# Gelus behind their additions, three products for the last batch's first pair, and a new order ahead of the branch and at the end

## The chip, the core and the metric

The kernel runs on one core of a Trainium2 chip. The time is the device time of one execution in microseconds (us). Before the change it is 1835.79 us, the median of three runs (1835.6 to 1835.98). One execution was also taken with the hardware profiler; that one took 1836.18 us, and its span, from the first to the last instruction, is 1834.4 us, so 1.8 us lie around the span. Five engines work side by side, each through its own instructions in order: PE (matrix products; PEld is its weight loading), DVE (vector work), ACT (activation functions), POOL (a second, slower vector engine), SP (which here only starts DMA transfers).

## The reference

The layer takes `x` of 4 batches, 2048 tokens and 256 features. What is computed:

```python
def step(h, qkv):                       # a linear recurrence over the tokens, per head (16 heads of 64)
    q, k, v = qkv
    h = alpha[None, :, :, None] * h + k[:, :, :, None] * v[:, :, None, :]
    return (h, jnp.einsum('bhi,bhij->bhj', q, h))
...
o = o * gate                            # gate = silu(xn @ Wg.T + bg)
y = o.reshape(batch, seq_len, D_INNER) @ WO.T + bO
...
x = _layernorm(x + attention(x))        # attention adds x once more
gf = _global_net(x.mean(axis=1))        # one number for each batch
out = x
for _ in range(3):                      # cycles
    tf = sigmoid(gelu(gelu(gelu(out @ w1 + b1) @ w2 + b2) @ w3 + b3) @ w4 + b4)     # one number a token
    coupling = 0.1 + adaptive_range * (0.7 * gf + 0.3 * tf - 0.5) * 2.0
    out = out + coupling * twist(out)   # twist: the four quarters of the features changed about, two with a minus
x = _layernorm(x + out)
```

Since the first product of the net is linear and the coupling is one number for each token, the kernel keeps u = out @ w1 and v = twist(out) @ w1, and a cycle becomes u + c v and v - c u, without a new product with w1.

## The kernel before, in words

**Ahead of the branch** (lines 230 to 329). Inputs are loaded; the bias of V is spread over all partitions by a product (line 248) that ACT copies out (line 249); a Sigmoid on ACT gives the decay factors (`powers[0]`, line 257), which DVE doubles up to 64 powers (`double`, lines 259 to 266); the first 512 tokens are normalised (`norm_steps`: `rs` on POOL, `xh` on DVE, transposes on PE line 182, ACT line 184); four products make V (`values_of`, line 199, added up on DVE line 203); the decay table `dtok` is transposed on PE (line 320) and copied on ACT (line 324); a one-element product (line 308) gives a flag that says whether a fast form of the recurrence is safe. Every engine reads the flag and branches. With these inputs the fast program runs.

**The fast program's loop** (`fast_program`). Batches of 2048 tokens are cut into 4 groups of 512 tokens, groups into 8 pairs of heads: 128 iterations, each in the same order on PE: 16 products for the outputs (`products`, line 1161), 16 for the state (`updates`, 646), three projections K, Q, g of the iteration after next (480), then a slot, then `inter` (1144), `all_scores` (573), `keys` (630), mostly one product for V (199), then a second slot. ACT copies the scores out (`copy_first`, line 589, "the A copies"), DVE copies a masked part (`copy_own`, line 594) and then `products` can start. On POOL each iteration has three multiplications (526, 536, 540) behind the Q projection.

**The slots** (`between`). Everything behind the recurrence is cut into steps and put into these slots by a planner when the program is built, from three clocks of its own (`clock`, `takes`) and the times written at each `step`: output projection and layer norm (`post`, queue `posts`), the global net (`nets`), and the coupling net (`feed_forward`, queue `couples`), which treats two groups at a time, s = 0 and 1. Small pieces of DVE work that belong to a product are put on the list `late` and issued at the end of a slot (`late_work`).

**The coupling net.** For all batches but the last, `both(s)` makes u and v with three products a half o instead of four (line 847): with J the twist, w1m = w1[0] + w1j[0], and the two differences of the halves of x1T formed on DVE (lines 841, 842), u and v are the first product (copied by ACT, line 848) plus the second and plus the third (DVE, lines 851, 852, in `adds`, on the list `late`). A step of its own, `gelu` (line 899), then issues two Gelus for both halves. In the last batch both pairs of groups take `first` (line 823): four products for u and four for v. `layer2` (line 905), w3 (940), w4 with a tanh (949, 952) follow; the result `cs` holds the coupling of each token on all partitions, and `turn` starts with c = cs ar3 + shift (868) and updates u and v. In the last batch's turn of cycle 1, DVE updates u (875, 878) while POOL updates v (876, 880). In cycle 2 only u is updated (886, 891).

**The end** (`the_end`). What is left of the queues after the loop is issued in the order of the string `AT_THE_END`: o is `post`, n the global net, p and q the last batch's first and second pair of groups, v the second pair's `first_twisted`. The last step of a pair mixes the token-wise couplings into coefficients (lines 970 to 993, a power on POOL line 987) and forms the output from them (ACT 1002, DVE 1016) for the DMA.

ACT's function tables are switched by an ACT_TABLE_LOAD, put in by the compiler where the next function is in another set: Gelu and Silu are, here; copies, Identity and Tanh need no switch of their own.

Of the kernel before, what the change touches and what calls it, by code (L numbers as in the profile page):

```python
# [49 lines left out]
P = 128  # L50
# [6 lines left out]
C = 64  # L57
# [10 lines left out]
ORDERED = {mybir.EngineType.PE, mybir.EngineType.DVE, mybir.EngineType.Activation, mybir.EngineType.Pool}  # L68


AT_THE_END = "qoopooqnnqnpqppvppqvqqqpqppqqpqqpqppqpppppqqqpqpqqqqpqpqpppqqpqpppqpppqqqpqqqqqq"
STAGES = ((2, 4), (8, 4), (32, 2))
EPS = 1e-5
LOW_ALPHA = 2.0**-5
# [4 lines left out]
def post_norm_layer(ctx: ExitStack, tc: tile.TileContext, a: dict, out: bass.AP):  # L79
# [152 lines left out]
    with ExitStack() as first:  # L232
        first.enter_context(tc.manual_schedule(engines=ORDERED))
        work = first.enter_context(tc.tile_pool(name="first", bufs=1))
        psum = first.enter_context(tc.tile_pool(name="firstp", bufs=4, space=bass.MemoryType.PSUM))

        def bank():
            return psum.tile([P, 512], F32, tag="pf", name="pf")


        diag = work.tile([P, HP, P], F32, tag="diag", name="diag")
        nc.vector.tensor_mul(
            diag, ident.unsqueeze(1).to_broadcast([P, HP, P]), b_in["V"].unsqueeze(2).to_broadcast([P, HP, P])
        )
        for half in range(2):
            hps = slice(half * (HP // 2), (half + 1) * (HP // 2))
            pt = bank()
            nc.tensor.matmul(pt, ones, diag[:, hps, :].rearrange("p j i -> p (j i)"), start=True, stop=True)
            nc.scalar.copy(bVt[:, half * 512 : (half + 1) * 512], pt)


        nc.vector.memset(up[:, :, 0:1], 1.0)
        nc.vector.memset(down[:, :, C : C + 1], 1.0)
        high = work.tile([P, 6], F32, tag="high", name="high")
        nc.vector.memset(high, 0.0)
        powers = [work.tile([P, HP, 1], F32, tag=f"apow{i}", name="apow") for i in range(C.bit_length())]
        nc.scalar.activation(powers[0], logit.unsqueeze(2), AF.Sigmoid)
# [26 lines left out]
        for i in range(3, C.bit_length() - 1):  # L284
            double(i)
        nc.vector.tensor_copy(up[:, :, C : C + 1], powers[-1])
        nc.vector.tensor_copy(down[:, :, 0:1], powers[-1])

        two = work.tile([P, HP, 2, C], F32, tag="two", name="two")
        nc.vector.tensor_copy(two, down[:, :, 1 : C + 1].unsqueeze(2).to_broadcast([P, HP, 2, C]))  # L290
        square(4, w_in["K"].rearrange("p k o -> p (k o)"))
        values_of(bank(), xn0, V0, 0, 0)

        peak = work.tile([P, 1], F32, tag="peak", name="peak")
        nc.vector.tensor_reduce(
            peak, w_in["Q"].rearrange("p k o -> p (k o)"), AX.X, ALU.max, apply_absolute_value=True
        )
# [12 lines left out]

        nc.vector.tensor_copy(kf[:, :, 0 : M + 1], down[:, :, C - M : C + 1])
        nc.vector.tensor_copy(qf[:, :, M:H], up[:, :, 0:M])
        nc.vector.reciprocal(kf[:, :, M + 1 : H], up[:, :, 1:M])
        nc.vector.reciprocal(qf[:, :, 0:M], down[:, :, C - M : C])
        values_of(bank(), xn0, V0, 0, 3)
        for half in range(2):
            hps = slice(half * (HP // 2), (half + 1) * (HP // 2))
            pt = bank()
            for j in range(HP // 2):
                nc.tensor.transpose(  # L320
                    pt[:, j * P : (j + 1) * P],
                    two[:, half * (HP // 2) + j].rearrange("p c s -> p (c s)"), ident,
                )
            nc.scalar.copy(dtok[:, hps, :].rearrange("p j i -> p (j i)"), pt)  # L324


        nc.gpsimd.iota(trow, pattern=[[1, C]], base=0, channel_multiplier=0)
        nc.gpsimd.iota(scol, pattern=[[0, 1]], base=0, channel_multiplier=1)
        nc.vector.tensor_scalar(scol, scol, C - 1, None, ALU.bitwise_and)
# [5 lines left out]
    def layer(fast, inside):  # L335
# [448 lines left out]
        def feed_forward(b, g0):  # L784
# [19 lines left out]
            gs = (g0, g0 + 1)  # L804
            u, v = [], []
            h1, h2 = {}, {}
            done = {}

            ctok = []
# [21 lines left out]
            def both(s):  # L831
# [11 lines left out]
                for o in range(2):  # L843
                    at = yield step("pe", 2.58, act=0.6)
                    ps = [pj() for _ in range(3)]
                    for w, r, q in ((w1m, o_, ps[0]), (w1[:, 0, :], diff, ps[1]), (w1j[:, 0, :], p_, ps[2])):
                        nc.tensor.matmul(q, w[:, o * P : (o + 1) * P], r, start=True, stop=True)  # L847
                    nc.scalar.copy(us[:, o, :], ps[0])

                    def adds(o=o, ps=ps):  # L850
                        nc.vector.tensor_add(vs[:, o, :], ps[1], us[:, o, :])
                        nc.vector.tensor_add(us[:, o, :], ps[2], us[:, o, :])

                    late.append(adds)
                    late.append(lambda: None)

                done["u", s] = at + 1.6
                done["v", s] = done["u", s]
                yield from gelu(s)

            def first_twisted():
                for s in range(2):
                    yield from first(s, w1j, v, "v")

            def turn(s, cycle):

# [2 lines left out]
                by_token(s, cycle - 1)  # L869
                if cycle == 1 and end:  # L870

                    done["u", s] = yield step("dve", 2.6)
                    ts = [(new("t"), SPARE[g0].pop(0)) for o in range(2)]
                    for o, (t0, t1) in enumerate(ts):
                        nc.vector.tensor_mul(t0, cs[s], v[s][:, o, :])
                        nc.gpsimd.tensor_mul(t1, cs[s], u[s][:, o, :])
                    for o, (t0, t1) in enumerate(ts):
                        nc.vector.tensor_add(u[s][:, o, :], u[s][:, o, :], t0)
                    for o, (t0, t1) in enumerate(ts):
                        nc.gpsimd.tensor_sub(v[s][:, o, :], v[s][:, o, :], t1)  # L880
                    return
                for o in range(2):
                    done["u", s] = yield step("dve", 1.3)
                    uo, vo = u[s][:, o, :], v[s][:, o, :]
# [10 lines left out]
            def gelu(s):  # L895
                done["h1", s] = yield step("act", 1.4, delay=0.2, at=lambda: done["u", s])
                for o in range(2):
                    h1[s, o] = new("h1")
                    nc.scalar.activation(h1[s, o], u[s][:, o, :], AF.Gelu, bias=b1[:, o : o + 1])

            def layer2(s):
                done["h2", s] = yield step("pe", 1.75, act=0.7, at=lambda: done.get(("h1", s), 0.0))
# [464 lines left out]
```

## Time and profile before

| what | value |
|---|---|
| time, median of 3 | 1835.79 us |
| the profiled execution's own time | 1836.18 us |
| its span | 1834.4 us |
| PE busy | 1781.6 us, 97% of the span |
| DVE busy | 1348.1 us, 73% |
| ACT busy | 755.7 us, 41% |
| POOL busy | 499.5 us, 27% |
| DMA | 20 GB/s over the span, 275 GB/s in the first 25 us |
| ACT_TABLE_LOAD | 118, of 1283 ns each |

Busy time is the sum over an engine's instructions. A row of the groups or of the timeline reads: line, engine, operation, the tile written and the tiles read, the shape, how often; in the timeline the start and the time taken stand in front, and behind it, in brackets, how long the engine had sat idle and what ended that. A product of 128x512 in float32 stands in the profile as two MATMULs, so "x4" is two products. PEclk is the share of TensorE's clock that was granted.

### The profile page before, as it was taken

What the parts mean: (1) busy time and instruction counts of PE and PEld (TensorE: products, weight loads), DVE (VectorE), ACT (ScalarE), POOL (GpSimd) and SP (SyncE); (2) the same over time, 40 slices, a digit from 0 to 9 for tenths busy, and PEclk for the clock granted to TensorE, in tenths of its full rate; (3) what the DMA queues carried; (4) which work ended last, traced back from release to release, by engine and by line L of the source; (5) the groups of instructions that cost most, each with busy time, mean ns of one, the idle gap of its engine ahead of it and who ended that gap; (6) DMA issues with size and microseconds to landing.
All of it is one profiled execution on the core that took longest, in us unless ns stands there. A gap on an engine that the chain in (4) does not pass through costs nothing.

```text
span 1834.4 us, 47983 instructions
## 1 busy us (share of the span) xinstructions
PE 1781.6 (97%) x20894; PEld 1026.4 (56%) x20894; DVE 1348.1 (73%) x3099; ACT 755.7 (41%) x1226; POOL 499.5 (27%) x452
## 2 busy tenths in 40 slices
PE   7999999999999999999999999999999999999985
PEld 3655555566555555565555555565555555555541
DVE  5677775767887868877688776877668876777467
ACT  3222324322454434543354334553355433453545
POOL 1332232223233222233132222222222232222242
PEclk9999999999999999999999999999999999999997
DMA  4000000000001000010001100010000100000002
GB/s 166 2 2 25 2 25 2 1 25 2 25 14 36 24 13 13 25 36 14 24 2 36 36 2 25 2 48 25 1 25 2 47 25 2 2 4 22 24 2 60
DMA packets 43819, 39.69 MB, mean 22 GB/s; under 512 B 20912, under 2 KB 39216, under 8 KB 43600
## 3 DMA queue, kind: packets, MB, share of 16 engines
q1 hardware_dynamic: 42320, 36.25, 6.2%
q8 instruction: 166, 2.72, 0.6%
q14 instruction: 53, 0.43, 0.1%
q10 hardware_dynamic: 1280, 0.29, 0.1%
HBM read 21.26 MB, written 15.27 MB: 20 GB/s over the span
## 4 chain that ended last, share of the span: by engine, by line
PE 89%; DVE 9%; issue 1%; ACT 1%; DMA 0%; POOL 0%; DVEq 0%; ACTq 0%
PE pj L480 34%; PE pj L683 12%; PE pj L199 11%; PE sc L573 4%; PE pj L905 4%; PE pu L1144 4%; PE pu L1161 4%; PE pj L630 4%; PE pj L847 3%; PE sc L646 3%; PE pj L940 1%; DVE states L656 1%; PE pj L823 1%; PE pj L949 1%; PE pj L710 1%
## 5 line engine op out<-in xcount | busy, mean ns | idle before, releaser
L526 POOL TENSOR_TENSOR qd<-QA,up 128x512 f32<-128x512 f32 x128 | 164.3, 1284 | 1159.6 <-ACT QA L498 1107.5
L494 ACT ACTIVATE KT<-pj,bK 128x512 f32<-128x512 f32 x128 | 87.9, 687 | 471.2 <-PE pj L480 471.2
L480 PE MATMUL pj<-xn,wK 128*128 128x512 f32 x512 | 253.8, 618 | 0.8 <-ACT dtok L324 0.8
L480 PE MATMUL pj<-xn,wg 128*128 128x512 f32 x512 | 240.6, 592 | 0.0
L480 PE MATMUL pj<-xn,wQ 128*128 128x512 f32 x512 | 240.6, 592 | 0.0
L656 DVE SCALAR_TENSOR_TENSOR states<-states,up,sc 128x64 f32<-128x64 f32 x768 | 215.8, 281 | 27.4
L199 PE MATMUL pj<-wV,xn 128*128 128x512 f32 x496 | 233.4, 593 | 0.0
L683 PE MATMUL pj<-wO,og 128*128 128x256 f32 x1024 | 231.9, 379 | 1.5 <-DVE og L1174 1.5
L683 PEld LDWEIGHTS pj<-wO,og 128*128 128x128 f32 x1024 | 194.3, 190 | 54.2 <-issue 27.7
L635 DVE TENSOR_TENSOR KE<-pj,dtok 128x512 f32<-128x512 f32 x128 | 88.1, 689 | 175.5 <-PE pj L630 175.5
L536 POOL TENSOR_TENSOR QF<-QA,qf 128x512 f32<-128x512 f32 x128 | 175.0, 1367 | 0.0
L480 PEld LDWEIGHTS pj<-xn,wQ 128*128 128x128 f32 x512 | 97.3, 190 | 122.4 <-issue 120.8
L480 PEld LDWEIGHTS pj<-xn,wg 128*128 128x128 f32 x512 | 97.3, 190 | 122.4 <-issue 110.2
L589 ACT COPY A<-sc 32x256 f32<-32x256 f32 x256 | 92.4, 361 | 147.0 <-PE sc L573 143.8
L498 ACT ACTIVATE QA<-pj,bQ 128x512 f32<-128x512 f32 x128 | 87.9, 687 | 140.5 <-PE pj L480 140.5
L480 PEld LDWEIGHTS pj<-xn,wK 128*128 128x128 f32 x512 | 86.7, 189 | 70.7 <-issue 62.2
L1161 PEld LDWEIGHTS pu<-A,V 64*64 64x64 f32 x4096 | 71.4, 134 | 84.9 <-DVE A L594 41.2
L199 PEld LDWEIGHTS pj<-wV,xn 128*128 128x128 f32 x496 | 84.6, 191 | 59.3 <-issue 59.3
L729 DVE TENSOR_TENSOR X<-pj,X 128x512 f32<-128x512 f32 x66 | 45.4, 688 | 96.9 <-PE pj L683 96.9
L510 ACT ACTIVATE gate<-pj,bg 128x512 f32<-128x512 f32 x128 | 88.0, 688 | 67.2 <-PE pj L480 62.7
L1174 DVE TENSOR_TENSOR og<-pu,gate 64x256 f32<-64x256 f32 x256 | 108.0, 422 | 6.3
L203 DVE TENSOR_TENSOR V<-pj,bVt 128x512 f32<-128x512 f32 x124 | 85.3, 688 | 34.4 <-PE pj L199 34.1
(222 smaller groups left out, 2721.2 us busy)
## 6 DMA issues: line engine op xcount, KB each, us to landing
X<-in_x SPq DMA_DIRECT2D x15, 512.0 KB, 3.8
out<-y SPq DMA_DIRECT2D x28, 256.0 KB, 2.1
kept<-X SPq DMA_DIRECT2D x13, 512.0 KB
x<-kept SPq DMA_DIRECT2D x13, 512.0 KB, 3.4
wV<-in_WV SPq DMA_DIRECT2D x1, 1024.0 KB, 6.2
wK<-in_WK SPq DMA_DIRECT2D x1, 1024.0 KB
wQ<-in_WQ SPq DMA_DIRECT2D x1, 1024.0 KB, 6.6
wg<-in_Wg SPq DMA_DIRECT2D x1, 1024.0 KB
```

What stands on the lines that cost most here:

```text
L199: nc.tensor.matmul(ps, xnT[:, k, i * P : (i + 1) * P], w_in["V"][:, k, half * 512 : (half + 1) * 512], start=(k == 0), stop=(k == KD - 1),)
L480: nc.tensor.matmul(ps, w_in[n][:, k, hp * P : (hp + 1) * P], xn[b, g][:, k, :], start=(k == 0), stop=(k == KD - 1),)
L494: nc.scalar.activation(kt, ps, AF.Identity, bias=b_in["K"][:, hp : hp + 1])
L510: nc.scalar.activation(gt, ps, AF.Silu, bias=b_in["g"][:, hp : hp + 1])
L526: nc.gpsimd.tensor_mul(qd, QA[it][:, :, 0:C], up[:, it[2], 1 : C + 1].unsqueeze(1).to_broadcast([P, NC, C]))
L536: nc.gpsimd.tensor_mul(qs[:, :, 0:C].rearrange("p c (n l) -> p c n l", l=H), qv.rearrange("p c (n l) -> p c n l", l=H), qf[:, hp, :].unsqu ...
L589: nc.scalar.copy(av[r, :, H:], pv[r, :, C : C + H])
L635: nc.vector.tensor_mul(ke, pt.rearrange("p (i x) -> p i x", i=NT), at(dtok, it[2], [P, NT, P]))
L656: nc.vector.scalar_tensor_tensor(o, before, up[:, hp, C : C + 1], u, ALU.mult, ALU.add)
L683: nc.tensor.matmul(ps[:, ii * D : (ii + 1) * D], og[b, g, hp][:, i * P : (i + 1) * P], wO[:, hp, :], start=(hp == hps[0]), stop=(hp == hps ...
L1161: tc.keep_in_program_order(nc.tensor.matmul(po[place(h, c), c, i * C : (i + 1) * C], V[r, i, m + h, :], A[r, h, i, :], start=False, stop=T ...
L1174: nc.vector.tensor_mul(ov[r, 1], pv[place(h, 1), 1], gv[r, 1])
```

## The change

Four things are done.

1. Ahead of the branch: the Sigmoid is issued first on ACT; the products for V, the peak of wQ and the transposes for `dtok` change places, so that the transposes stand ahead of the flag's product and the fourth product of V behind it.
2. In `both`, the two additions are two entries of the list `late`, and the one that ends u issues its Gelu directly behind; the step `gelu` after `both` is gone.
3. The last batch's first pair takes `both` too (`if fast and not second`).
4. In the last batch's turn of cycle 1, POOL does nothing more: DVE writes c v + u into a free tile (`new_u`), and the update of v, in place of u's old tile, is a step of its own, `turn_v`, which comes after both `layer2` of that cycle. `AT_THE_END` is a new string of 84 letters (80 before).

```diff
-AT_THE_END = "qoopooqnnqnpqppvppqvqqqpqppqqpqqpqppqpppppqqqpqpqqqqpqpqpppqqpqpppqpppqqqpqqqqqq"
+AT_THE_END = "pqovoqonnpnppqpppvqpqpqpppqqpqqqpppqpppqppqpqqpqpqqqqpqqqpqpqqpqpqpqppqpppqpqqqqqqqq"
...
+        powers = [work.tile([P, HP, 1], F32, tag=f"apow{i}", name="apow") for i in range(C.bit_length())]
+        nc.scalar.activation(powers[0], logit.unsqueeze(2), AF.Sigmoid)
...
-        powers = [work.tile([P, HP, 1], F32, tag=f"apow{i}", name="apow") for i in range(C.bit_length())]
-        nc.scalar.activation(powers[0], logit.unsqueeze(2), AF.Sigmoid)
...
-        values_of(bank(), xn0, V0, 0, 0)
+        for i in range(2):
+            values_of(bank(), xn0, V0, 0, i)
...
-        values_of(bank(), xn0, V0, 0, 1)
...
         values_of(bank(), xn0, V0, 0, 2)
-        pt = bank()
-        nc.tensor.matmul(pt[0:1, 0:1], good, ones[:, 0:1], start=True, stop=True)
-        nc.vector.tensor_scalar(flag, pt[0:1, 0:1], P - 0.5, None, ALU.is_ge)
...
-        values_of(bank(), xn0, V0, 0, 3)
         for half in range(2):
...
             nc.scalar.copy(dtok[:, hps, :].rearrange("p j i -> p (j i)"), pt)
+        pt = bank()
+        nc.tensor.matmul(pt[0:1, 0:1], good, ones[:, 0:1], start=True, stop=True)
+        nc.vector.tensor_scalar(flag, pt[0:1, 0:1], P - 0.5, None, ALU.is_ge)
...
+        values_of(bank(), xn0, V0, 0, 3)
...
-                    def adds(o=o, ps=ps):
+                    def add_v(o=o, ps=ps):
                         nc.vector.tensor_add(vs[:, o, :], ps[1], us[:, o, :])
+
+                    def add_u(o=o, ps=ps):
                         nc.vector.tensor_add(us[:, o, :], ps[2], us[:, o, :])
-
-                    late.append(adds)
-                    late.append(lambda: None)
-
-                done["u", s] = at + 1.6
-                done["v", s] = done["u", s]
-                yield from gelu(s)
+                        h1[s, o] = new("h1")
+                        nc.scalar.activation(h1[s, o], us[:, o, :], AF.Gelu, bias=b1[:, o : o + 1])
+                        takes("act", 0.7, max(clock["dve"], clock["pe"] + 0.2) + 0.65)
+
+                    late.append(add_v)
+                    late.append(add_u)
+
+                done["v", s] = at + 1.6
+                done["h1", s] = at + 2.5
...
+            def u_of(s, o):
+                return new_u.get((s, o), u[s][:, o, :])
...
                 if cycle == 1 and end:
 
-                    done["u", s] = yield step("dve", 2.6)
-                    ts = [(new("t"), SPARE[g0].pop(0)) for o in range(2)]
-                    for o, (t0, t1) in enumerate(ts):
-                        nc.vector.tensor_mul(t0, cs[s], v[s][:, o, :])
-                        nc.gpsimd.tensor_mul(t1, cs[s], u[s][:, o, :])
-                    for o, (t0, t1) in enumerate(ts):
-                        nc.vector.tensor_add(u[s][:, o, :], u[s][:, o, :], t0)
-                    for o, (t0, t1) in enumerate(ts):
-                        nc.gpsimd.tensor_sub(v[s][:, o, :], v[s][:, o, :], t1)
+                    done["u", s] = yield step("dve", 2.8)
+                    for o in range(2):
+                        new_u[s, o] = SPARE[g0].pop(0)
+                        nc.vector.tensor_mul(new_u[s, o], cs[s], v[s][:, o, :])
+                        nc.vector.tensor_add(new_u[s, o], new_u[s, o], u[s][:, o, :])
                     return
...
+            def turn_v(s):
+
+                yield step("dve", 2.8)
+                for o in range(2):
+                    uo, vo = u[s][:, o, :], v[s][:, o, :]
+                    nc.vector.tensor_mul(uo, uo, cs[s])
+                    nc.vector.tensor_sub(vo, vo, uo)
...
-                    if fast and not end:
+                    if fast and not second:
                         yield from both(s)
...
                     for s in range(2):
                         yield from gelu(s)
                         yield from layer2(s)
+                    if cycle == 1:
+                        for s in range(2):
+                            yield from turn_v(s)
```

More of the change, by code (lines that the diff above doesn't have):

```diff
@@ L306, in post_norm_layer @@
         values_of(bank(), xn0, V0, 0, 2)
-        pt = bank()
-        nc.tensor.matmul(pt[0:1, 0:1], good, ones[:, 0:1], start=True, stop=True)
-        nc.vector.tensor_scalar(flag, pt[0:1, 0:1], P - 0.5, None, ALU.is_ge)
[L311 to L314, printed above, removed]
-        values_of(bank(), xn0, V0, 0, 3)
         for half in range(2):
@@ L324, in post_norm_layer @@
             nc.scalar.copy(dtok[:, hps, :].rearrange("p j i -> p (j i)"), pt)
+        pt = bank()
+        nc.tensor.matmul(pt[0:1, 0:1], good, ones[:, 0:1], start=True, stop=True)
+        nc.vector.tensor_scalar(flag, pt[0:1, 0:1], P - 0.5, None, ALU.is_ge)
+        nc.vector.tensor_copy(kf[:, :, 0 : M + 1], down[:, :, C - M : C + 1])
+        nc.vector.tensor_copy(qf[:, :, M:H], up[:, :, 0:M])
+        nc.vector.reciprocal(kf[:, :, M + 1 : H], up[:, :, 1:M])
+        nc.vector.reciprocal(qf[:, :, 0:M], down[:, :, C - M : C])
+        values_of(bank(), xn0, V0, 0, 3)
         nc.gpsimd.iota(trow, pattern=[[1, C]], base=0, channel_multiplier=0)
@@ L806, in feed_forward @@
             h1, h2 = {}, {}
+            new_u = {}
             done = {}
@@ L883, in turn @@
                     done["u", s] = yield step("dve", 1.3)
-                    uo, vo = u[s][:, o, :], v[s][:, o, :]
+                    uo, vo = u_of(s, o), v[s][:, o, :]
                     t0 = new("t")
@@ L898, in gelu @@
                     h1[s, o] = new("h1")
-                    nc.scalar.activation(h1[s, o], u[s][:, o, :], AF.Gelu, bias=b1[:, o : o + 1])
+                    nc.scalar.activation(h1[s, o], u_of(s, o), AF.Gelu, bias=b1[:, o : o + 1])
+            def turn_v(s):
[4 more added lines that the diff above has]
+                    nc.vector.tensor_sub(vo, vo, uo)
             def layer2(s):
```

## The prediction, made before the changed kernel ran

> **What bounds the kernel now.** I read the page's busy times first, then a table of stretches, then the timeline of the three stretches in which PE is not full. The page:
>
> ```profile
> span 1834.4 us, 47983 instructions
> PE 1781.6 (97%) x20894; PEld 1026.4 (56%) x20894; DVE 1348.1 (73%) x3099; ACT 755.7 (41%) x1226; POOL 499.5 (27%) x452
> ```
>
> PE has 52.8 us without work. The stretches say where (the second figure is the length, then PE, PEld, DVE, ACT, POOL, the granted clock, DMA):
>
> ```profile
> 0.00:25.00 25.00, 15.09 (x39) 7.19 (x39) 16.17 (x59) 9.98 (x22) 2.70 (x13) 1.00 0.79 275
> ...
> 44.00:1700.00 1656.00, 1641.45 (x19905) 957.90 (x19904) 1240.44 (x2831) 673.34 (x1082) 453.04 (x408) 1.00 0.06 17
> ...
> 1750.00:1781.00 31.00, 28.21 (x84) 12.16 (x84) 20.43 (x37) 16.24 (x31) 12.30 (x8) 1.00 0.02 2
> 1781.00:1820.00 39.00, 28.51 (x68) 9.46 (x68) 31.41 (x55) 20.86 (x35) 17.10 (x11) 0.87 0.08 15
> 1820.00:1834.40 14.40, 0.00 (x0) 0.00 (x0) 9.21 (x44) 6.31 (x13) 1.68 (x1) 0.56 0.45 151
> ```
>
> 9.9 us lie ahead of the branch, 14.6 us are spread over 1656 us of loop, 27.7 us lie behind 1750. In the loop only fewer products or fewer pauses count; ahead of the branch and at the end the chain of waits counts. Ahead of the branch (timeline of ACT, DVE, POOL and PE):
>
> ```profile
> 8.43 0.58 ACT L249 COPY bVt<-pf 128x512 f32<-128x512 f32 x1 [1.12 <-PE pf L248]
> 9.03 1.28 ACT L257 ACT_TABLE_LOAD   x1
> 10.32 0.21 ACT L257 ACTIVATE apow<-logit 128x8 f32<-128x8 f32 x1
> ...
> 11.58 1.38 DVE L159 TENSOR_SCALAR xh<-X,mv,rs 128x256 f32<-128x256 f32 x4
> ...
> 7.92 1.02 POOL L147 TENSOR_TENSOR rs<-ve,neghalf 128x4 f32<-128x4 f32 x1 [6.48 <-DVE ve L145]
> ...
> 24.97 1.95 PE L480 MATMUL pj<-xn,wK 128*128 128x512 f32 x4 [0.77 <-ACT dtok L324]
> ```
>
> `xh` has its `rs` at 8.94 but stands on DVE behind three doublings (1.1 us) that wait for the Sigmoid, which waits behind two copies for a second table load; and the loop starts when ACT's last `dtok` copy is done. A pause in the loop:
>
> ```profile
> 670.97 0.42 DVE L154 BATCH_NORM_STATS2 st<-X 128x6 f32<-128x256 f32 x1
> ...
> 674.67 0.69 PE L1161 MATMUL pu<-A,V 64*64 64x64 f32 x32 [0.77 <-DVE A L594]
> ```
>
> Layer-norm statistics (2.4 us) stand on DVE behind the additions of `both`, and so `copy_own` and the products are late. The end (DVE, then POOL, then PE):
>
> ```profile
> 1774.50 1.49 DVE L868 TENSOR_SCALAR cs<-cs,ar,sh 128x512 f32<-128x512 f32 x1
> 1776.03 2.37 DVE L875 TENSOR_TENSOR t<-cs,v 128x512 f32<-128x512 f32 x2
> 1778.32 3.43 DVE L878 TENSOR_TENSOR u<-u,t 128x512 f32<-128x512 f32 x2
> ...
> 1801.97 0.69 DVE L891 TENSOR_TENSOR u<-u,t 128x512 f32<-128x512 f32 x1
> ...
> 1776.45 3.08 POOL L876 TENSOR_TENSOR V<-cs,u 128x512 f32<-128x512 f32 x2 [0.74 <-ACT V L829]
> 1779.49 3.39 POOL L880 TENSOR_TENSOR v<-v,V 128x512 f32<-128x512 f32 x2
> ...
> 1795.19 3.78 PE L905 MATMUL pj<-h,w 128*128 128x512 f32 x4 [2.65 <-ACT h L899]
> ...
> 1803.39 1.98 PE L905 MATMUL pj<-h,w 128*128 128x512 f32 x4
> ```
>
> While POOL updates v, an addition on DVE takes 1.7 us; the same addition alone takes 0.69. A turn of one group takes 7.17 us (1774.50 to 1781.67) beside POOL; in cycle 2, without POOL, 3.24 (1797.43 to 1800.67). The four turns run from 1768.27 to 1796.0 without a break and are the chain there.
>
> **Ahead of the branch.** The Sigmoid comes behind the first table load, at 6.05 instead of 10.32, and the second load (1.28) is gone. DVE's doublings then run behind `ve`, 7.77 to 8.86, and `xh` starts at 8.96, 2.6 us earlier; wV is there (issued 1.25, 6.2 to landing), so the first V product starts at 11.2 (13.81). Then DVE sets the pace: two V additions to 16.35, the peak of wQ 2.28 (wQ lands at 14.1), 0.6 for the rest: `good` at 19.3 (21.08). The flag's product and the fourth V product (4 x 0.43) end at 21.6, its addition stands behind flag and reciprocals (1.95) and ends at 22.6; `dtok` is long copied. K starts between 22.0 and 22.7: **-2.6 us**, bounds -1.5 (the pause at the branch grows by one) and -3.2. The 1 MB loads are hidden: the last of them, wg, was issued at 7.88, and DMA traffic falls off at 17.
>
> **The loop.** Products: none fewer until the last batch. There the first pair takes 12 instead of 16, each 0.88 (3.53 for four): 3.5 us of a full PE, counted in the end below. The Gelu stands on ACT ahead of the A copies in 13 of 28 cases (new order: u copy, load, Gelu, A copies). From the K projection's start: projections 5.35, three products 2.58, so the addition that ends u is done at 8.6 to 9.5 and the Gelu (0.72) at 9.3 to 10.3, while the scores are ready at 5.35 + 2.58 + 1.29 = 9.2. The A copies are late by up to 1.1 us, `copy_own` ends at 11.8, and the products stand at 13.8 or later, since a slot with other products (2.58 of `both`, or 0.95 + 1.8) or V comes between: spare 2.0 in six cases, 3.1 in six, 1.2 in one. Cost nothing; without that cover 13 x 1.1 = 14 us. Behind the waiting Gelu stand K's and Q's copies in the other 15 cases, due 2 us later.
>
> The five pauses of 0.77 (batch after batch, by the statistics behind `both`) go, because the same chain now reaches `both` half an iteration earlier and that slot holds only the statistics: -3.9. What is late next: in three iterations four turn operations stand ahead of `copy_own`; with 1.1 to 1.76 each beside POOL the products are 0.2 late by my layout, 1.2 at worst: +0.6 (to +3.6). I take **-3.3 us**, bounds -4 and +2.
>
> There are 133 table loads for 118: 15 x 1.283 = 19.2 us on an ACT that is busy 41%. In the trace a load runs ahead of the wait (load at 1705.95, then 1.58 idle for the product) and the next function starts 0.02 behind a load. [...]
>
> **The end.** Up to 1706.89 both orders are the same. From there the new order needs, on a full PE: twice products, updates and projections (1.09 + 5.35), twice `inter` to `keys` (1.78), three times three products (2.6), 1.09 more: the last batch's 12 output products start at 1732.2, where before they started at 1740.16. Adding 5.57, 1.29, 2.6, one layer2 1.8 and `products`, then DVE's gate (1.45 idle, as before), the last four output products start at 1745.6 (1751.08): -5.5, of it 3.5 for products saved and 1.9 for a layer2 that moves behind. The shift `sh` is then ready at 1764.1 (1768.23), 4.1 earlier, since more of the second pair's first products stand ahead of the global net.
>
> From there DVE is the chain, all alone at 0.55 + 4 x 0.69 with overlap, 3.25 a turn and 2.66 for a group's v: first pair's turns 6.5, their v 5.3, a wait of 1.3 for the second pair's tanh, turns 6.5, first pair's cycle 2 6.5, second pair's v 5.3 (its tanh tile must be free before cycle 2's is written), its cycle 2 6.5: 37.9 us. Before: 4 turns 27.9, 1.4 wait, 6.5, 0.3, 6.6, so 42.7. That is -4.8. From the last u to the last coefficients (1810.9 to 1819.66, 8.8): Gelu 0.9, layer2 1.3, Gelu 0.7, w3 0.7, then h3 behind two output activations of the first pair 2.3, token product 1.1, tanh 0.3: 7.3, so -1.4. The last 14.7 us are the same work. Sum -4.1 - 4.8 - 1.4 = -10.3.
>
> PE's clock takes something back. Half clock was granted for 3.4 and 6.9 us from 1787.6 on, after pauses of 2.5 and 2.65 us; a layer2 then took 3.45 and 3.78 instead of 1.98. In my layout PE pauses 2.8 us near 1796 and is idle 6 of the 10 us up to the last layer2. If that layer2, w3 and the token product run at half clock, it costs 1.5 to 2.7: +1.8 taken, none to +4 as bounds. [...] **-8.5 us**, bounds -10.3 and -5.
>
> **The sum.** -2.6 - 3.3 - 8.5 = -14.4. Against the profiled execution 1836.18 gives 1821.8; the median of the runs stands 0.39 lower, so **1821.4 us**.
>
> **The rivals.**
> *The v updates only change places* (0.15): turn_v stands on DVE in the chain twice (10.6 us); if the second pair's tanh comes late as well, the chain is as long as before and 4.8 are lost: 1826.2. For it: DVE's chain has only 1.3 us of wait in my layout. Against: 7.17 against 3.25 + 2.66 a group.
> *Gelu and load in front of the A copies* (0.08): were the load to start only with the Gelu's operand, the A copies were late by up to 1.1 + 1.28 = 2.4: 0.4 over the spare in six cases and 1.2 in one, 3.6 in sum; with the gain of 3.3 lost to `copy_own`, which stands behind them, 1828.3. The rows of loads speak against it.
> *The start doesn't come* (0.07): the loop's first bank waits for V's last addition, and the branch takes as long behind it as a later flag would: 1824.
> *A cold end, slower than before* (0.04): with every engine waiting in turn, PE stays at half clock from 1763 on. It has 33 us of work there and 10 us of pauses, so the end comes 23 us later: 1843. It decides against the change from 28 of these 33 us cold; before, 9.1 of them were.
>
> **How the numbers follow.** My forecast has 0.62, 1818 to 1825. Two in ten left out, the range is 1817.5 to 1828.5. About 0.2% (3.7 us) is what a measurement of this kernel can tell from no change. All but the cold end and a remainder of 0.04, in which several bounds meet, end faster: faster 0.92, same 0.04, slower 0.04.
>
> **What would show it.** The K projection's start near 22.4; no POOL multiplication and DVE operations of 0.69 behind 1750; the waits of products for `copy_own` without the five of 0.77; `sh` near 1758 in the new time (1764.1 less 5.9 of the parts before). Wrong would be: waits of products for ACT's A copies, a lower granted clock in the last 60 us, or a last chain that hangs on DVE's v updates.

## The result and the profile after

The changed kernel takes 1825.81 us in the median of five runs, the kernel before 1835.79: 10.0 us less, ratio 0.9948 with a 95% interval of 0.9937 to 0.9959. The forecast was 1821.4 us in a range of 1817.5 to 1828.5: the sign and the range are right, and 4.4 us of the 14.4 forecast did not come. Two executions of the kernels below took 2051 and 2297 us at a granted clock of 0.85 and 0.75; the medians given here are of the others.

The page of the changed kernel:

```profile
span 1824.0 us, 47978 instructions
PE 1772.4 (97%) x20886; PEld 1023.8 (56%) x20886; DVE 1359.2 (75%) x3127; ACT 772.8 (42%) x1237; POOL 474.9 (26%) x436
```

PE has 51.6 us without work, before 52.8: of the 10.4 us that the span is shorter, 9.2 are busy time of PE, and the waits as a whole are hardly fewer. Not all of the 9.2 is work taken out: the products saved are 3.5, and half clock, at which a `layer2` took 3.45 and 3.78 us instead of 1.98, was granted for 10.2 us ahead of the last products before and for 3.4 now. The table of stretches (length, then PE, PEld, DVE, ACT, POOL busy, the granted clock, the DMA share and GB/s):

```profile
0.00:25.00 25.00, 16.78 (x44) 8.02 (x44) 16.94 (x62) 9.35 (x22) 2.75 (x13) 1.00 0.82 275
...
44.00:1700.00 1656.00, 1638.55 (x19904) 956.74 (x19903) 1244.97 (x2827) 694.34 (x1098) 454.24 (x408) 1.00 0.06 17
...
1750.00:1781.00 31.00, 28.84 (x83) 12.11 (x82) 18.90 (x40) 18.43 (x35) 1.01 (x1) 1.00 0.08 18
1781.00:1820.00 39.00, 21.15 (x60) 7.90 (x60) 33.32 (x99) 24.64 (x43) 3.32 (x2) 0.85 0.18 49
```

The start is fuller (PE 16.78 us of 25 instead of 15.09). POOL is empty at the end, 1.01 and 3.32 us instead of 12.30 and 17.10. But in the loop PE has 17.45 us without work, where before it had 14.55: there the change lost.

Where the time went is best read from when the same instruction starts in both traces. The projection of K starts 128 times; the chain at the end has `sh` and the last coefficients:

| mark | before | after | difference | of this stretch alone | forecast |
|---|---|---|---|---|---|
| first K projection | 24.97 | 22.78 | -2.19 | start: -2.2 | -2.6 |
| K projection of iteration 124 of 0 to 127 | 1682.64 | 1681.79 | -0.85 | loop: +1.3 | -3.3 |
| `sh` | 1768.01 | 1764.41 | -3.60 | products of the end: -2.75 | -4.1 |
| last coefficients | 1819.66 | 1809.38 | -10.28 | DVE's chain and the tail: -6.7 | -4.4 |
| end of the span | 1834.33 | 1823.96 | -10.37 | last outputs: -0.1 | 0 |

So nearly the whole miss is the loop: +1.3 instead of -3.3. The end came to -9.5 instead of -8.5.

The lines that answer to those of before. Ahead of the branch (timeline of ACT, DVE and PE; start, time taken, engine, line):

```profile
4.82 1.28 ACT L241 ACT_TABLE_LOAD   x1 [4.82 <-DMA X<-in_x]
7.35 0.21 ACT L241 ACTIVATE apow<-logit 128x8 f32<-128x8 f32 x1 [1.25 <-DMA logit<-in_alpha_logit]
...
9.12 1.39 DVE L159 TENSOR_SCALAR xh<-X,mv,rs 128x256 f32<-128x256 f32 x4 [0.22 <-POOL rs L147]
...
21.91 0.61 DVE L203 TENSOR_TENSOR V<-pf,bVt 128x512 f32<-128x512 f32 x1
...
22.78 1.95 PE L480 MATMUL pj<-xn,wK 128*128 128x512 f32 x4 [1.10 <-DVE sw L416]
```

The second table load is gone and `xh` starts at 9.12 instead of 11.58, as worked out; the K projection starts 0.26 us behind the last addition of V (end 22.52), after a pause of 1.10 us. The row names the cast `sw`, which ends just ahead of it, as what ended the pause; a run below shows that the projection does not need that cast.

In the loop the five pauses of 0.77 us are gone, and six new ones have come. This is the first of three pairs (DVE, then POOL, then PE):

```profile
682.88 1.76 DVE L890 TENSOR_TENSOR t<-cs,v 128x512 f32<-128x512 f32 x1
684.57 1.76 DVE L893 TENSOR_TENSOR t<-cs,u 128x512 f32<-128x512 f32 x1
686.37 1.11 DVE L895 TENSOR_TENSOR u<-u,t 128x512 f32<-128x512 f32 x1
687.40 0.68 DVE L897 TENSOR_TENSOR v<-v,t 128x512 f32<-128x512 f32 x1
688.00 0.68 DVE L635 TENSOR_TENSOR KE<-pj,dtok 128x512 f32<-128x512 f32 x1
...
694.76 0.68 DVE L722 TENSOR_REDUCE mj<-X 128x4 f32<-128x512 f32 x1
695.48 0.68 DVE L723 TENSOR_SCALAR mj<-mj 128x4 f32<-128x4 f32 x1
696.19 1.20 DVE L724 TENSOR_TENSOR vj<-mj 128x4 f32<-128x4 f32 x1
697.42 0.65 DVE L725 TENSOR_TENSOR vj<-sq,vj 128x4 f32<-128x4 f32 x1
...
682.81 1.28 POOL L526 TENSOR_TENSOR qd<-QA,up 128x512 f32<-128x512 f32 x1 [8.03 <-ACT QA L498]
684.06 1.72 POOL L536 TENSOR_TENSOR QF<-QA,qf 128x512 f32<-128x512 f32 x1
685.75 1.18 POOL L540 TENSOR_TENSOR QF<-QA,up 128x256 f32<-128x256 f32 x1
695.04 1.09 POOL L526 TENSOR_TENSOR qd<-QA,up 128x512 f32<-128x512 f32 x1 [8.12 <-ACT QA L498]
696.09 1.28 POOL L536 TENSOR_TENSOR QF<-QA,qf 128x512 f32<-128x512 f32 x1
697.33 0.73 POOL L540 TENSOR_TENSOR QF<-QA,up 128x256 f32<-128x256 f32 x1
...
689.37 0.69 PE L1176 MATMUL pu<-A,V 64*64 64x64 f32 x32 [1.26 <-DVE A L594]
700.56 0.69 PE L1176 MATMUL pu<-A,V 64*64 64x64 f32 x32 [1.09 <-DVE A L594]
```

Four operations of a turn stand on DVE ahead of `decayed` (KE) and `copy_own`, beside POOL's three multiplications, and take 5.3 us instead of 2.7. In the next iteration two turn products stand there behind three tiny layer-norm operations, which take 0.68, 1.20 and 0.65 us instead of some 0.17 each. Both times `copy_own` is late, and the products wait 1.26 and 1.09 us. The same pair stands at 1131.56 and 1142.75, and at 1573.82 and 1585.01.

The end (DVE):

```profile
1764.66 0.55 DVE L876 TENSOR_SCALAR cs<-cs,ar,sh 128x512 f32<-128x512 f32 x1
1765.24 0.69 DVE L883 TENSOR_TENSOR V<-cs,v 128x512 f32<-128x512 f32 x1
...
1777.24 0.55 DVE L876 TENSOR_SCALAR cs<-cs,ar,sh 128x512 f32<-128x512 f32 x1 [0.69 <-ACT cs L967]
...
1801.38 0.69 DVE L895 TENSOR_TENSOR carry<-carry,t 128x512 f32<-128x512 f32 x1
```

From 1764.66 to 1802.07 DVE pauses once, for 0.69 us. Every operation takes 0.54 to 0.69.

### The profile page after: what moved, and what is told of

Same layout as the page of the kernel before. It is cut to its first block, busy times and chain, and to the rows that moved or that the text cites. A ratio compares the mean times of both kernels' runs of the same rounds, so it can differ in the third digit from the quotient of the medians.

```text
span 1824.0 us, 47978 instructions
## 1 busy us (share of the span) xinstructions
PE 1772.4 (97%) x20886; PEld 1023.8 (56%) x20886; DVE 1359.2 (75%) x3127; ACT 772.8 (42%) x1237; POOL 474.9 (26%) x436
## 4 chain that ended last, share of the span: by engine, by line
PE 87%; DVE 12%; issue 1%; DMA 0%; ACT 0%; POOL 0%; DVEq 0%; ACTq 0%; POOLq 0%
PE pj L480 33%; PE pj L683 12%; PE pj L199 10%; PE sc L573 4%; PE pu L1159 4%; PE pu L1176 4%; PE pj L848 4%; PE pj L917 4%; PE pj L630 4%; PE sc L646 3%; DVE states L656 2%; PE pj L955 1%; DVE X L159 1%; DVE og L1189 1%; PE pj L824 1%
## 5 line engine op out<-in xcount | busy, mean ns | idle before, releaser
L635 DVE TENSOR_TENSOR KE<-pj,dtok 128x512 f32<-128x512 f32 x128 | 88.1, 688 | 163.9 <-PE pj L630 163.8
```

What stands on the lines that cost most here:

```text
L635: nc.vector.tensor_mul(ke, pt.rearrange("p (i x) -> p i x", i=NT), at(dtok, it[2], [P, NT, P]))
```

## The experiments

### The three parts alone

First the kernel before with one part of the change each. Ahead of the branch:

```diff
+        nc.scalar.activation(powers[0], logit.unsqueeze(2), AF.Sigmoid)
...
-        nc.scalar.activation(powers[0], logit.unsqueeze(2), AF.Sigmoid)
...
-        nc.tensor.matmul(pt[0:1, 0:1], good, ones[:, 0:1], start=True, stop=True)
...
             nc.scalar.copy(dtok[:, hps, :].rearrange("p j i -> p (j i)"), pt)
+        pt = bank()
+        nc.tensor.matmul(pt[0:1, 0:1], good, ones[:, 0:1], start=True, stop=True)
...
+        values_of(bank(), xn0, V0, 0, 3)
```

> The kernel before with the new order ahead of the branch alone. If the trace of the changed kernel is read rightly, the first K projection starts near 22.8 us instead of 24.97, nothing later gives it back, and the time falls by 2.2 to about 1833.6 us. Rival: the loop's waits take it back, 1835.8 us.

Measured: 1833.88 us against 1835.66 (ratio 0.9993, interval 0.9984 to 1.0002). In the trace the first K projection is 2.25 us earlier, and the shift is -2.18 in the middle of the loop and -1.84 at its end. The gain is there in the trace and passes through the loop; in the time it is 1.8 us, which the interval does not tell from none. Why it is hard to see: with the old start the first K projection comes at 24.97 us in the kernel before and at 24.27 in the run with the new end alone (below), whose start is the same.

The additions and the Gelu of `both` alone:

```diff
-                    late.append(adds)
-                    late.append(lambda: None)
...
-                yield from gelu(s)
...
+                    late.append(add_v)
+                    late.append(add_u)
```

> The kernel before with the new additions and Gelus of `both` alone (three batches); start and end as before. By the prediction: five pauses of 0.77 us vanish, 0.6 comes back, 1832.5 us. By the theory from the trace of the changed kernel: the same five vanish (-3.9), but in three iterations pairs the turns of the coupling net and the small layer-norm operations stand ahead of copy_own beside POOL, two pauses of 1.26 and 1.09 us each time (+7.1), some small ones go (-1.3): +1.9, 1837.7 us.

Measured: 1837.09 us, ratio 1.0011 (1.0002 to 1.002): slower by 1.4, near the second number and on the other side of the first. The trace of this kernel shows the pauses of the changed kernel, to the hundredth:

```profile
691.56 0.69 PE L1165 MATMUL pu<-A,V 64*64 64x64 f32 x32 [1.26 <-DVE A L594]
702.75 0.69 PE L1165 MATMUL pu<-A,V 64*64 64x64 f32 x32 [1.09 <-DVE A L594]
```

K projections are 0.03 us earlier than before in iteration 40 and 1.31 later at the end of the loop. So this part, in the loop, is a loss.

The end alone (the old additions and Gelu step in all batches but the last, the old start; the lines are against the changed kernel):

```diff
+                    late.append(add_v if end else adds)
+                    late.append(add_u if end else lambda: None)
...
+                if not end:
+                    done["u", s] = at + 1.6
+                    yield from gelu(s)
```

> The kernel before with the new end alone: three products for the last batch's first pair, the turn without POOL, the new order; the other batches keep the old Gelu step, the start is the old one. By the prediction -8.5: 1827.3 us. By the trace of the changed kernel (no clock loss on the path) -10.1: 1825.7 us.

Measured: 1828.31 us, ratio 0.9959 (0.9946 to 0.9973): -7.4. `sh` and the 37.6 us of DVE's chain behind it are those of the changed kernel (the first coefficients stand 37.59 us behind `sh` here, 37.58 there). What differs is the tail: 8.8 us from the first coefficients to the last, where the changed kernel has 7.4. That is a matter of the clock, and is taken up below. The three parts alone sum to -1.8 + 1.4 - 7.4 = -7.8, the change to -10.0; by the two profiles 1.4 of the difference is this tail; the rest, 0.8, is no more than the start differs by between executions.

### What makes the new pauses

Two changes to the changed kernel, each aimed at the six pauses. In the first only the order is touched, in the slots of six iterations:

```diff
-        def between(dve, act, free=False):
+        def between(dve, act, free=False, tight=0.0):
...
-                    elif start + time <= clock["pe"] + (dve if kind == "dve" else act):
+                    elif start + time <= clock["pe"] + (dve - tight if kind == "dve" else act):
...
-                between(1.9, 1.5, not then)
+                between(1.9, 1.5, not then, 1.2 if n in (49, 50, 81, 82, 113, 114) else 0.0)
```

> The changed kernel, but in six slots of the loop (iterations 49, 50, 81, 82, 113, 114) the planner has 1.2 us less of DVE time, so that the turn there issues two operations instead of four in the first and the two turn products leave the second; the rest of the order is the same. If those operations in front of copy_own make the six pauses, they go: -7.0, about 1818.8 us. Rival: DVE is short of time there anyway and the pause only moves to the next slot, 1825 us.

Measured: 1817.98 us (1817.59 to 1820.33), ratio 0.9908 (0.9893 to 0.9923) against 0.9948 for the changed kernel: 7.8 us faster than it. In the loop the K projections gain 7.4 us on the changed kernel, and none of the six pauses is left. The lines of the first pair (DVE, then PE, where no idle time is noted):

```profile
682.06 1.76 DVE L890 TENSOR_TENSOR t<-cs,v 128x512 f32<-128x512 f32 x1
683.75 1.77 DVE L893 TENSOR_TENSOR t<-cs,u 128x512 f32<-128x512 f32 x1
685.60 0.69 DVE L635 TENSOR_TENSOR KE<-pj,dtok 128x512 f32<-128x512 f32 x1
...
694.04 1.19 DVE L724 TENSOR_TENSOR vj<-mj 128x4 f32<-128x4 f32 x1
...
695.84 0.68 DVE L635 TENSOR_TENSOR KE<-pj,dtok 128x512 f32<-128x512 f32 x1
...
687.21 0.70 PE L1176 MATMUL pu<-A,V 64*64 64x64 f32 x32
697.25 0.69 PE L1176 MATMUL pu<-A,V 64*64 64x64 f32 x32
```

The operations that stay are as slow as before, but there are two fewer in each slot, and nothing waits. The rival, that the pause moves to the next slot, falls: that slot holds the same number of DVE operations as in the changed kernel, beside output products, and no pause stands there.

In the second the order stays and POOL is taken away:

```diff
+            if its.index(it) in (51, 52, 83, 84, 115, 116):
+                nc.gpsimd.memset(qd, 0.0)
+                qdec[it] = qd
+                return
             nc.gpsimd.tensor_mul(
                 qd, QA[it][:, :, 0:C], ...
```

(and the same for QF)

> The changed kernel, but in the six iterations with the new pauses (51, 52, 83, 84, 115, 116) POOL's three multiplications of Q are left out (POOL writes zeros instead, so the outputs of these iterations are not computed); DVE's work and its order stay. If the pauses come from DVE standing beside POOL (operations of 0.69 us taking 1.1 to 1.76, small ones of 0.16 taking 0.65 to 1.2), they vanish and the time is about 1818.7 us, as with the turns spread. Rival: the number of operations in front of copy_own is enough for the pauses, POOL or not: 1825.8 us.

Measured: 1818.07 us, ratio 0.9903 (0.9886 to 0.9919). The same operations in the same order:

```profile
683.44 0.68 DVE L898 TENSOR_TENSOR t<-cs,v 128x512 f32<-128x512 f32 x1
...
685.37 0.68 DVE L905 TENSOR_TENSOR v<-v,t 128x512 f32<-128x512 f32 x1
686.98 0.69 DVE L643 TENSOR_TENSOR KE<-pj,dtok 128x512 f32<-128x512 f32 x1 [0.93 <-PE pj L638]
...
694.90 0.16 DVE L732 TENSOR_TENSOR vj<-mj 128x4 f32<-128x4 f32 x1
```

KE now waits 0.93 us for PE instead of PE for `copy_own`. So it takes both: that many operations ahead of `copy_own`, and POOL beside them. Either one taken away is worth the same: 7.4 and 7.5 us in the loop by the K projections, 7.8 and 7.7 in the time.

### The end: products, POOL and DVE

Four products a half again for the last batch's first pair, in the steps of the changed kernel:

```diff
+                    if end:
+                        pu, pv = pj(), pj()
+                        for w, q in ((w1, pu), (w1j, pv)):
+                            for k in range(KD):
+                                nc.tensor.matmul(
+                                    q, w[:, k, o * P : (o + 1) * P], x1[:, k, :], start=(k == 0), stop=(k == KD - 1)
+                                )
...
```

> The changed kernel, but the last batch's first pair gets its u and v by four products a half o instead of three, in the same steps of the same order; ACT copies both and takes the Gelu from the bank, the two differences and the additions on DVE are left out there. If PE is the bound up to `sh`, the four products of 0.88 us more come back whole: +3.5, about 1829.3 us, with `sh` 3.5 later. Rival: a wait swallows them, since the global net and the tanh end later than the products anyway: 1826.5 us or less.

Measured: 1829.45 us, ratio 0.9968 (0.9956 to 0.998), 3.6 above the changed kernel; `sh` at 1767.93 instead of 1764.41. Of these 3.5 us, 0.3 are a later start and 0.1 comes from the loop: from the K projection of iteration 124 to `sh` it is 85.77 us instead of 82.62, 3.15 more for four products of 0.88. PE is the bound up to `sh`, and nearly all of the products saved there counts.

POOL's update of v back in the turn:

```diff
+                    ts = [(new("t"), SPARE[g0].pop(0)) for o in range(2)]
+                    for o, (t0, t1) in enumerate(ts):
+                        nc.vector.tensor_mul(t0, cs[s], v[s][:, o, :])
+                        nc.gpsimd.tensor_mul(t1, cs[s], u[s][:, o, :])
...
             def turn_v(s):
                 yield step("dve", 2.8)
-                for o in range(2):
...
```

> The changed kernel with the turn of cycle 1 at the end as it was: POOL updates v beside DVE, which updates u in place; the step `turn_v` is empty, the order is the same. If DVE alone is faster since POOL slows each of its additions from 0.69 to 1.7 us, the turns take 4 x 7 instead of 4 x 3.25 + 4 x 2.66 us: 1764.7 + 28 + 0.7 + 13 gives the last u at 1806.4 instead of 1802.1, +4.3, about 1830.1 us. Rival (v updates on DVE only change places): DVE's own v updates cost the chain as much as the contention did, 1826 us.

Measured: 1836.61 us, ratio 1.0004 (0.9995 to 1.0013): 10.8 above the changed kernel, more than twice what was expected. The direction was right, the size was not. DVE's lines:

```profile
1765.56 0.55 DVE L876 TENSOR_SCALAR cs<-cs,ar,sh 128x512 f32<-128x512 f32 x1
1766.14 2.37 DVE L883 TENSOR_TENSOR t<-cs,v 128x512 f32<-128x512 f32 x2
1768.43 3.43 DVE L886 TENSOR_TENSOR u<-u,t 128x512 f32<-128x512 f32 x2
...
1793.80 1.48 DVE L876 TENSOR_SCALAR cs<-cs,ar,sh 128x512 f32<-128x512 f32 x1
...
1805.30 0.55 DVE L876 TENSOR_SCALAR cs<-cs,ar,sh 128x512 f32<-128x512 f32 x1 [3.99 <-ACT cs L967]
```

The four turns take 28.2 us, as worked out (1765.56 to 1793.80). But then DVE stands still for 3.99 us. The second pair's turns end at 1793.8 instead of 1783.7, the last of its Gelus, layer2, w3 and tanh come behind them, and only the first pair's cycle 2 (7.5 us) lies beside these; in the changed kernel 5.3 us of v updates lie there as well. A layer2 takes 3.78 us here (from 1793.01), as one did at half clock in the kernel before; but ACT's next Gelus wait for DVE's u (2.20 and 0.61 us idle), not for that layer2. From `sh` to the last coefficients it is 53.94 us instead of 44.97: 9.0 of the 10.0 us between the two profiled executions (1835.85 and 1825.81); 0.9 more is the start, which came later in this one. So the v updates on DVE do two things: they take away the contention, and they stand where DVE would have to wait.

### The pause ahead of the branch, and the clock near the end

In the changed kernel PE pauses 1.32 us before the flag's product and 1.10 before the first K projection, and the fourth V product stands between the two. Moved ahead of the flag's product:

```diff
+        values_of(bank(), xn0, V0, 0, 3)
         pt = bank()
         nc.tensor.matmul(pt[0:1, 0:1], good, ones[:, 0:1], start=True, stop=True)
...
-        values_of(bank(), xn0, V0, 0, 3)
```

> The changed kernel with the fourth V product ahead of the flag's product, in PE's pause of 1.3 us there. In the changed kernel the first K projection starts 0.26 us behind the last V addition (22.52), not behind the branch. If that addition is what it waits for, it starts at 21.6 to 21.9 instead of 22.8: about 1824.8 us. Rival: it waits for the reciprocals and casts behind the flag on DVE, which come no earlier: 1825.8 us.

Measured: 1825.86 us, ratio 0.9946 (0.9932 to 0.9959). From `good`, the operand of the flag's product, to the first K projection it is 2.49 us instead of 3.51, so the 1.0 is there: the projection starts 1.11 us ahead of the end of the cast `sw`, and what it waited for in the changed kernel was V's last addition, which now ends before the flag is written. (PE's wait for DVE there ended at 22.6, 0.1 behind the addition and 0.9 behind PE's own last product.) But the time did not move. The last coefficients stand 46.35 us behind `sh` instead of 44.97: the tail of the run with the end alone.

That tail is the clock. Stretches of the changed kernel, cut where its clock changes (columns as in the table of stretches above):

```profile
1794.50:1797.80 3.30, 1.15 (x10) 0.97 (x8) 3.20 (x6) 1.70 (x4) 0.00 (x0) 1.00 0.00 1
1797.80:1801.20 3.40, 2.88 (x4) 1.12 (x4) 3.30 (x6) 1.19 (x2) 0.00 (x0) 0.50 0.08 1
```

The same of the kernel with the end alone:

```profile
1794.70:1800.00 5.30, 2.43 (x13) 1.43 (x12) 5.13 (x9) 2.89 (x5) 0.00 (x0) 1.00 0.05 1
1800.00:1806.80 6.80, 5.41 (x6) 1.41 (x6) 4.41 (x21) 1.91 (x3) 1.64 (x1) 0.50 0.04 1
```

In the one, half clock is granted for 3.4 us and falls on the last but one layer2, which is hidden behind DVE; in the other for 6.8 us and on the last one, which is on the chain. The two last layer2 of the changed kernel (PE):

```profile
1798.32 3.40 PE L917 MATMUL pj<-h,w 128*128 128x512 f32 x4 [0.99 <-ACT h L903]
1803.11 1.98 PE L917 MATMUL pj<-h,w 128*128 128x512 f32 x4 [1.39 <-ACT h L903]
```

And the last one of the kernel with the end alone:

```profile
1803.19 3.77 PE L924 MATMUL pj<-h,w 128*128 128x512 f32 x4 [1.39 <-ACT h L910]
```

Of the seven kernels with these instructions at the end, three profiles show a tail of 7.4 us (the changed kernel, the turns spread, four products), three of 8.8 (the end alone, V early, and both of the next run's edits) and one of 9.7 (POOL's zeros). What decides it is where the half clock falls. In the three with 7.4 it begins 33.4, 33.8 and 34.3 us behind `sh` and lasts 3.4 us; in the one with 9.7 it begins 34.6 behind and lasts 10.2; in the three with 8.8 it begins 35.2 to 35.4 behind and lasts 6.8. The changes of clock near the end lie 3.41, 3.41, 6.83 and 20.48 us apart in the kernel before and 3.41 and 10.24 in the changed kernel; where the first of them stands against the program differs from one profiled execution to the next. Both together (turns spread, fourth V product early):

> The kernel of the run with the turns spread over more slots (1817.98 us), with the fourth V product ahead of the flag's product as well: if both gains add, 1817.0 us, otherwise 1818.0 us.

Measured: 1819.47 us; its profile has the tail of 8.8 us, so the time says nothing on the start. Then three products that nobody uses, in PE's pauses near the end (an unused bank, wK as both operands):

```diff
+        def keep_warm(n):
+            w = w_in["K"]
+            nc.tensor.matmul(two_banks("sc", 1)[:, 0, 0:n], w[:, 0, 0:P], w[:, 0, 0:n], start=True, stop=True)
...
                         yield from layer2(s)
+                        if cycle == 2 and second and s == 0:
+                            keep_warm(512)
```

> The kernel with the turns spread, with three unused products on PE in its pauses near the end (0.88 us behind the first pair's last w3, 0.44 behind its token product, 0.88 behind the second pair's first last layer2). If the half clock near the end comes from these pauses, it is gone between the first of them and the last layer2, that layer2 takes 1.98 us in every execution, and the slower executions (2 us above the others) vanish: 1817.5 us and less spread. Rival: the half clock comes anyway, or costs nothing: 1818.0 us with the same spread.

> The same three unused products, and the fourth V product ahead of the flag's product as well. If the 1.0 us that the first K projection comes earlier behind the flag's operand was only hidden by a half clock at the end, it shows now: 1816.6 us. Rival: the start's gain is lost elsewhere, 1817.6 us.

Measured: 1817.14 us (1816.98 to 1818.54) with the turns spread, ratio 0.9902 (0.9886 to 0.9919), and 1817.59 (1816.11 to 1817.86) with V early as well. Half a miss: in the first the half clock still comes, for 3.4 us, and makes the last but one layer2 3.40 us long; in the second it does not come before the last products. In neither profile is the last layer2 slow. That the longer tail is gone for good is not shown by one profile and four times of each. The early V product stays inconclusive too: 1.0 us behind `good` in every trace, but `good` itself comes between 18.0 and 19.9 us in the six traces with and without it, with nothing changed ahead of `good`, and the medians show no gain.

The kernel with the turns spread and the unused products has the lowest median here: 8.7 us below the changed kernel, 18.5 below the kernel before as measured beside it. What is certain of that is the 7.8 of the spread turns.

## Why the prediction came out as it did

**Ahead of the branch** (-2.6, came -2.2). Every step of the chain came as worked out: Sigmoid first, `xh` 2.5 earlier, the flag's operand at 19.4 (19.3 forecast). The 0.4 is the last term, the pause at the branch, for which the bound was one microsecond: it grew from 0.77 to 1.10, and it ends with V's last addition. That was the rival "the start doesn't come" in small: the first bank of the loop does wait for that addition, but the addition came with the rest.

**The loop** (-3.3, came +1.3). This is the step that failed. The five pauses vanish as forecast. The Gelu ahead of the A copies costs nothing, also as forecast: no pause names ACT's A copies, and the 15 more table loads are seen nowhere but in ACT's busy time, 772.8 us for 755.7. What failed is the term for what is late next, "in three iterations four turn operations stand ahead of `copy_own`; with 1.1 to 1.76 each beside POOL the products are 0.2 late by my layout, 1.2 at worst: +0.6 (to +3.6)". The three iterations were the right ones and the durations too (1.76, 1.76, 1.11, 0.68), but the lateness is 1.26, the bound taken for the worst and not the 0.2 of the layout: 3.8 us. And a second iteration behind each was not in the sum at all: two turn products behind the three small layer-norm operations, which beside POOL take 2.5 us instead of 0.5, 1.09 late: 3.3 us. The prediction does not mention them. At their durations without POOL, some 0.17 us for a small one, they make no pause, as the run with POOL's zeros shows. Six pauses of 7.1 us stand against five of 3.9. By that the loop should be 3.2 longer, and PE's idle time in it did grow by 2.9; the K projections say +1.3. In the kernel with this part alone, which also says +1.3, PE's busy time fell by 1.6 with the same number of instructions. Counted there from the start of one product to the start of the next, 3.4 us are lost behind V's products, where the pauses stand, and 1.6 come back at `inter` and 1.0 at the transposes; the few tenths left are spread. Why those became shorter is open.

**The end, up to `sh`** (-4.1, came -2.75). The products saved are worth nearly what was said: 3.6 in the time and 3.15 in the trace, for 3.5. The layout put the last batch's 12 output products 7.96 us earlier and they are 7.4 earlier against the loop; the rest of the 1.35 slips in the waits behind them. No single step explains it.

**The end, DVE's chain** (-4.8, with the tail -1.4 and the clock +1.8; came -6.7). Taken apart, the chain came at -5.3, the tail at -1.5 and the clock at 0. DVE goes from `sh` to the last u in 37.4 us, 37.9 were forecast, and waits 0.69 where 1.3 was said. The rival "the v updates only change places" is refuted twice, by the 0.69 and by the run with POOL back. That run says that the reason was incomplete: the contention is 28 us against 13 + 10.6, and the other half of the 9 us is cover for the second pair's tanh.

**The clock** (+1.8, came 0 in the profile). The layer2 at half clock was said to be on the chain. In the profile of the changed kernel it is the one before. In four of the six other profiles of the same end it is the last one, at 1.4 us in three of them and 2.3 in the fourth. So the term is about right for some executions and 0 for others, by where the half clock falls; one profiled execution cannot price it.

That the total lay in the range is partly luck of signs: the loop missed by 4.6 to the bad side, the end by 1.0 to the good one. The range of the loop's own term, -4 to +2, held it.

## What to carry to other kernels

Where an order is planned ahead, look for the slots that an edit fills, not for those it empties: read the new order up to the next operation with a deadline, and cost everything ahead of it at the durations beside POOL (here 1.11 to 1.76 us for 0.69), the tiny operations too (0.65 to 1.20 for 0.17). A bound worked out "at worst" from such rows is a better guess than a layout that just fits. When a move from one engine to another pays, ask what it now covers as well as what it no longer disturbs; only the undoing showed that half of the gain.

## What the hardware showed that was not expected

Beside POOL's multiplications DVE's operations of a turn do not seem to run slower, but to stand until POOL's instruction ends. In the lines above POOL's multiplications end at 684.09, 685.78 and 686.93, DVE's operations at 684.64, 686.33 and 687.47, each 0.55 us behind. A 128x4 operation of 0.17 us ends at 696.16, where POOL's ends at 696.13, the next at 697.39 (697.37), the next at 698.07 (698.05). The same holds in the whole trace of the changed kernel: 43 operations of turns (`t`, `u`, `v`) start while one of POOL's three multiplications has more than 0.1 us to run, and each ends 0.545 to 0.552 us behind its end. KE (L635), which reads one of its inputs from PE's banks, starts so 23 times and takes its 0.68 to 0.69 us each time; the layer norm's statistics (L154) start so 60 times and take 0.39 to 0.40. What sets these apart is not shown. With POOL writing zeros, none of the turn's operations waits, but the zeros are written late and overlap only the last of them (`v`), by 0.21 us; it takes its 0.68 us.

In the changed kernel the half clock came behind pauses of PE shorter than the 2.51 and 2.65 us of the kernel before: ahead of it PE worked 1.15 us of 3.3, with pauses of 1.68 and 0.99. With the unused products it still came once, behind a stretch of 3.4 us with 2.44 busy. It lasted 3.4, 6.8 or 10.2 us. What brings it on is not shown.
